# A transformer block on one core: the first LayerNorm in two halves of its slots, with shift, scale and w1 loaded and used in two halves of their columns

## The chip, the core and the metric

The kernel runs on one of the eight cores of a Trainium2 chip. The core has five engines with queues of their own: TensorE (PE, with weight loads shown as PEld), VectorE (DVE), ScalarE (ACT), GpSimd (POOL) and SyncE (SP), which here only issues DMAs. The metric is the device time of one execution in microseconds, as the median of several executions. All tensors are float32.

## The reference

A conditioned block: six rows per batch entry are made from the condition, and two residual branches use them as shift, scale and gate. The input x has 2 batch entries of 2048 rows with 512 features; the hidden width of the second branch is 1024.

```python
emb = jnp.dot(jax.nn.silu(t), ada_w) + ada_b
shift_msa, scale_msa, gate_msa, shift_mlp, scale_mlp, gate_mlp = jnp.split(emb, 6, axis=-1)
norm = _ln(x) * (1.0 + scale_msa[:, None]) + shift_msa[:, None]
h = jax.nn.gelu(jnp.dot(norm, ssm_w1) + ssm_b1, approximate=False)
ssm_out = jnp.dot(h, ssm_w2) + ssm_b2
x = x + gate_msa[:, None] * ssm_out
norm2 = _ln(x) * (1.0 + scale_mlp[:, None]) + shift_mlp[:, None]
hf = jax.nn.gelu(jnp.dot(norm2, ff_w1) + ff_b1, approximate=True)
ff_out = jnp.dot(hf, ff_w2) + ff_b2
x = x + gate_mlp[:, None] * ff_out
```

## The kernel before

**Tiling.** The 4096 rows are cut into 8 blocks of 512. A block holds 128 partitions with 4 rows each; the four rows of a partition are its slots. Features are cut into four chunks k of 128. The products of a block are formed in the way of Strassen and Winograd: seven products P1 to P7 of halves instead of eight, with sums of halves of the operands made beforehand by DVE or POOL. `group` (L376) issues the products in a given order; after each, `after` drains PSUM, and then the hooks hung on that product are issued. The schedule is manual: each engine works in the order in which the code issues to it.

**The beginning, by engine.** The first 16 us belong to block 0, before any product of a block can run.

- SP loads in this order: x of block 0 in two pieces, ada_0 (shift), ada_1 (scale), w1, ada_2 (gate), w2, b2, x of block 1, ada_3, ada_4, fw1 (L232 to L249). ada_0 to ada_4 are blocks of 512 columns of ada_w. ACT's queue loads the small rows with the condition and the biases.
- PE runs idle products (L774) and turns the small rows into columns (colsT). When ada_0 and ada_1 have landed, it forms shift and scale (`modulation`, L253, products at L261): for each, 16 small products, four at a time on column groups of the array. Between them and P1 stand 16 transposes (L494) of the normalized block.
- DVE forms the statistics of the four slots (L425, L426), copies colsT (L779), adds 1 to the scale's bias (L790), makes `pick` (L793) and `pick_bc` (L800), a selection matrix that the gate's product uses, and computes four small operations for the scales (L442 to L445) after POOL's two (L434, L436). It then turns and finishes shift (L271, L275), normalizes slots 1 and 3 (L469), finishes scale, and modulates chunks 1 and 3 (L510). ACT normalizes slots 0 and 2 (L465) and modulates chunks 0 and 2 (L508). Normalized rows go into the tile `blocks`, modulated ones into nT.
- POOL forms four sums of quarters of w1 (`sums_of_first` through `weight_of_first`, L311): w_s[1], then the quarter 21 in place, then w_s[0], then w_s[2]. DVE forms four sums of nT in the same way (`summed`, L530, L311): two before P1's drain, the third after P1, the fourth after P2.

**Block 0's first products** stand in the order P1, P2, P5, P6, P3, P7, P4 (L843). P1 uses the quarter 11 of w1 and P2 the quarter 12, both in the first half of w1's columns; P1 needs chunks 0 and 1 of nT, P2 chunks 2 and 3. P5 needs POOL's second sum and DVE's second sum, P6 POOL's third, P3 POOL's fourth. After P2, PE forms the gate's rows (`rows_of_gates`, L284, from ada_2); DVE adds the bias to them (grows, L293). After P5, PE multiplies grows by pick_bc (pgate, `make_gate`, L299); DVE multiplies b2 (gb, L830) and then w2 (L359) with pgate. DVE's order in this stretch is: sums 1 and 2, drain of P1 (forms, L565), sum 3, drain of P2 (L571), grows, sum 4, drain of P5, gb, w2, drain of P6.

Of the kernel before, what the change touches and what calls it, by code (L numbers as in the profile page):

```python
# [36 lines left out]
F32 = mybir.dt.float32  # L37
AF = mybir.ActivationFunctionType
ALU = mybir.AluOpType
EPS = 1e-06  # L40
# [100 lines left out]
def kernel(  # L141
# [16 lines left out]
    nc = tc.nc  # L158
    P = 128
    B, N, D = x.shape  # L160
    H = fw1.shape[1]
    KD = D // P
    KH = H // P
    C = 4
    TB = C * P
# [5 lines left out]
    const = ctx.enter_context(tc.tile_pool(name="const", bufs=1))  # L171
# [3 lines left out]
    small = ctx.enter_context(tc.tile_pool(name="small", bufs=3))  # L175
    ps_t = ctx.enter_context(tc.tile_pool(name="ps_t", bufs=2, space=bass.MemoryType.PSUM))
    ps_g = ctx.enter_context(tc.tile_pool(name="ps_g", bufs=2, space=bass.MemoryType.PSUM))
# [7 lines left out]
    G = 32  # L185
# [3 lines left out]
    R_COND, R_ADA = 0, B * KD  # L189
# [3 lines left out]
    def big_tile(name):  # L193
        return big.tile([P, KD, D], F32, tag="big", name=name)
# [3 lines left out]
    def load_x(i, pieces=1):  # L198
        xs[i] = big_tile(f"x_{i}")
        for s in range(pieces):  # L200
            c = slice(s * C // pieces, (s + 1) * C // pieces)
            nc.sync.dma_start(out=xs[i][:, c, :], in_=x_blk[i][:, c, :])

    ada = {}

    def load_ada(g):
        ada[g] = big_tile(f"ada_{g}")
        nc.sync.dma_start(
            out=ada[g], in_=ada_w[:, g * D : (g + 1) * D].rearrange("(k p) n -> p k n", p=P)
        )  # L210

    def load_w(name, w, t=None, eng=nc.sync):
        if t is None:
            t = const.tile([P, w.shape[0] // P, w.shape[1]], F32, tag=name, name=name)
        eng.dma_start(out=t, in_=w.rearrange("(k p) n -> p k n", p=P))
        return t
# [13 lines left out]
    ident = const.tile([P, P], F32, tag="ident", name="ident")  # L230
    make_identity(nc, ident)
    load_x(0, 2)  # L232
    load_ada(0)
    load_ada(1)
    w1_sb = load_w("w1", w1)
    load_ada(2)

    nc.gpsimd.memset(brows[:, :2, :], 0.0)
    for n, g in enumerate((2, 5)):
        nc.scalar.dma_start(  # L240
            out=brows[:B, n, :], in_=ada_b[g * D : (g + 1) * D].unsqueeze(0).to_broadcast([B, D])
# [6 lines left out]
    load_ada(4)  # L248
    fw1_sb = load_w("fw1", fw1)  # L249

    mods = {}

    def modulation(g0, part):  # L253


        g = g0 + part
        pa = ps_g.tile([P, D], F32, tag="x", name=f"pada_{g}")
        w = ada[g].rearrange("p k (n m q) -> p k m n q", n=KD, q=G)
        for k in range(KD):
            for m in range(P // G):  # L260
                nc.tensor.matmul(  # L261
                    pa[m * G : (m + 1) * G, :P],
                    silu[:, k, :],
                    w[:, k, m],
                    start=(k == 0),
                    stop=(k == KD - 1),
                    tile_position=(0, m * G),
                    skip_group_check=True,
                )
        turned = pa[:, P : 2 * P]  # L270
        nc.vector.transpose(turned, pa[:, :P])  # L271
        turned = turned.rearrange("p (n q) -> p n q", n=KD)
        m = const.tile([P, KD, B], F32, tag=f"mod_{g0}_{part}", name=f"mod_{g0}_{part}")
        bias = colsT[:, R_ADA + g * KD : R_ADA + (g + 1) * KD]
        nc.vector.tensor_tensor(m, turned[:, :, :B], bias.unsqueeze(2).to_broadcast([P, KD, B]), ALU.add)  # L275
        mods[g0, part] = m

    gate, gate_rows = {}, {}

# [23 lines left out]
    def quarters(lo, hi, a, b):  # L303

        return {"11": lo[:, :, a], "12": hi[:, :, a], "21": lo[:, :, b], "22": hi[:, :, b]}
# [7 lines left out]
    def sums_of_first(q, s, eng, cut=1):  # L313

        return [
            lambda: cut_sum(eng, s[1], q["11"], q["21"], ALU.subtract, cut),
            lambda: cut_sum(eng, q["21"], q["21"], q["22"], ALU.add, cut),
            lambda: cut_sum(eng, s[0], q["21"], q["11"], ALU.subtract, cut),
            lambda: cut_sum(eng, s[2], q["12"], s[0], ALU.subtract, cut),
        ]  # L320
# [10 lines left out]
    def first_operands(q, s):  # L331
        return {"P1": q["11"], "P2": q["12"], "P3": s[2], "P4": q["22"], "P5": q["21"], "P6": s[0], "P7": s[1]}
# [4 lines left out]
    def thirds(t):  # L337
        return [t[:, j] for j in range(3)]

    def weight_of_first(name, w_sb):  # L340

        K, M = w_sb.shape[1], w_sb.shape[2]
        tile_s = const.tile([P, 3, K // 2, M // 2], F32, tag=f"{name}_s", name=f"{name}_s")
        s = thirds(tile_s)
        lo, hi = w_sb[:, : K // 2, :], w_sb[:, K // 2 :, :]
        q = quarters(lo, hi, slice(0, M // 2), slice(M // 2, M))
        return first_operands(q, s), sums_of_first(q, s, nc.gpsimd), tile_s
# [64 lines left out]
    class Norm:  # L412
# [17 lines left out]
        def scales(self, on_dve=False):  # L430

            n, v = self.name, nc.gpsimd
            ve = small.tile([P, C], F32, tag="ve", name=f"ve{n}")
            v.tensor_scalar(ve, self.mv[:, :, 1], EPS, None, ALU.add)  # L434
            r = small.tile([P, C], F32, tag="r", name=f"r{n}")
            v.tensor_tensor(r, ve, minus_half, ALU.pow)  # L436
            e = small.tile([P, C], F32, tag="e", name=f"e{n}")
            self.rstd = small.tile([P, C], F32, tag="rstd", name=f"rstd{n}")
            self.nmr = small.tile([P, C], F32, tag="nmr", name=f"nmr{n}")
            if on_dve:  # L440
                v = nc.vector
                v.tensor_tensor(e, r, ve, ALU.mult)  # L442
                v.scalar_tensor_tensor(e, e, -0.5, r, ALU.mult, ALU.mult)
                v.scalar_tensor_tensor(self.rstd, e, 1.5, r, ALU.add, ALU.mult)
                v.scalar_tensor_tensor(self.nmr, self.mv[:, :, 0], -1.0, self.rstd, ALU.mult, ALU.mult)  # L445
                return
            v.tensor_tensor(e, r, r, ALU.mult)
            v.tensor_tensor(e, e, ve, ALU.mult)
            v.tensor_scalar(e, e, -0.5, 1.5, ALU.mult, ALU.add)
            v.tensor_tensor(self.rstd, r, e, ALU.mult)  # L450
            v.tensor_tensor(self.nmr, self.mv[:, :, 0], self.rstd, ALU.mult)
            v.tensor_scalar(self.nmr, self.nmr, -1.0, None, ALU.mult)  # L452

        def blocks(self):
            return work.tile([P, C, KD, C, Q], F32, tag="blocks", name=f"blocks{self.name}")
# [293 lines left out]
    def run(ops):  # L749
        for op in ops:  # L750
            op()
# [4 lines left out]
    n1 = {0: Norm(0, 1), 1: Norm(1, 1)}  # L756

    minus_half = const.tile([P, C], F32, tag="minus_half", name="minus_half")
# [6 lines left out]
    colsT = const.tile([P, ROWS], F32, tag="colsT", name="colsT")  # L765
# [5 lines left out]
    for n in range(IDLE):  # L771
# [3 lines left out]
            idle, ident, ident.unsqueeze(1).to_broadcast([P, C, P]), start=True, stop=True  # L775
        )

    run(n1[0].stats())
    nc.vector.tensor_copy(colsT, pt[:, :ROWS])  # L779


    nc.scalar.activation(
# [1 line left out]
        colsT[:, R_COND:R_ADA].rearrange("p (b k) -> p b k", b=B),  # L784
        AF.Silu,
    )

    for g in (1, 4):
        rows_g = colsT[:, R_ADA + g * KD : R_ADA + (g + 1) * KD]
        nc.vector.tensor_scalar(rows_g, rows_g, 1.0, None, ALU.add)  # L790

    pick = const.tile([P, B], F32, tag="pick", name="pick")
    nc.vector.tensor_reduce(  # L793
# [4 lines left out]
    )  # L798
    pick_bc = const.tile([P, B, P], F32, tag="pick_bc", name="pick_bc")
    nc.vector.tensor_copy(pick_bc, pick.unsqueeze(2).to_broadcast([P, B, P]))  # L800
    n1[0].scales(on_dve=True)

    w1_ops, w1_sums, _ = weight_of_first("w1", w1_sb)
    run(w1_sums)
    modulation(0, 0)
    for c in range(C):
        n1[0].normal(c, nc.vector if c % 2 else None, on_pe=True)
    modulation(0, 1)
    pts = {}

    def transposed(k):
        pts[k] = n1[0].transpose(k, ps_g.tile([P, TB], F32, tag="yv"[k % 2], name=f"pt1_0_{k}"))

    for k in range(KD):
        transposed(k)
    for k in range(KD):
        n1[0].modulate(k, pts[k], nc.vector if k % 2 else None)
    n1_sums = n1[0].summed(nc.vector)
    run(n1_sums[:2])
    load_ada(5)  # L820
    fw2_sb = load_w("fw2", fw2)
    gb, hA = {2: b2_bc}, {}
# [15 lines left out]
    st = n1[1].stats()  # L838
    hook(hooks, ("P5",), [ssm_gate, gb2_0] + biases(0, b2_bc) + fold2(0, 1))
    hook(hooks, ("P6",), fold2(1, 7))  # L840
    hook(hooks, ("P3", "P7"), st[:2])
    hook(hooks, ("P7",), [lambda: modulation(3, 0)])
    hA[0] = First(0, n1[0].ops, hooks, ("P1", "P2", "P5", "P6", "P3", "P7", "P4"), hA_0)  # L843
    w2_ops = found["w2"][0]
# [9 lines left out]
    st = n2[0].stats()  # L854
# [17 lines left out]
    n1_sums = n1[1].summed(nc.vector)  # L872
# [21 lines left out]
    st = n1[2].stats()  # L894
# [221 lines left out]
```

## Time and profile before

| | us |
|---|---|
| median of 3 runs | 600.43 |
| lowest and highest | 600.42 and 600.75 |
| the profiled execution, whole | 600.48 |
| its span, first to last instruction | 598.7 |
| PE busy in the span | 591.4 |
| DVE busy | 374.3 |
| POOL busy | 399.1 |
| ACT busy | 218.8 |

The span is 1.8 us shorter than the profiled execution, which is near the median. The granted TensorE clock was 0.999 of full speed. In the lines of the profile a timeline row gives the start in us, the length in us, the engine, the line of the code, the operation, and the tiles as out<-in; a bracket gives how long the engine was idle before and what released it. A row of the chain of waits gives start, length and what the chain ran through; it is followed backwards from the last instruction, at each step to what released it.

### The profile page before, as it was taken

The numbers are of one execution on the slowest core, as the hardware profiler recorded it, in microseconds if no ns is written. First come the engines' busy times: TensorE is split into PE (matmuls) and PEld (weight loads), VectorE is DVE, ScalarE is ACT, GpSimd is POOL, SyncE is SP. The second block draws the span as 40 slices with busy tenths as digits, with TensorE's granted clock in tenths as the row PEclk, the third lists the DMA queues.
The fourth block names the chain that finished last, engine by engine and source line by source line (L and its number), as shares of the span: only waits on it lengthen the run. The fifth ranks groups of instructions, "written<-read, shape, count | busy, mean of one in ns | idle before, by whom it ended". The sixth has DMA issues, their size and how long they took to land.

```text
span 598.7 us, 8148 instructions
## 1 busy us (share of the span) xinstructions
PE 591.4 (99%) x2827; PEld 510.1 (85%) x2827; DVE 374.3 (63%) x638; ACT 218.8 (37%) x363; POOL 399.1 (67%) x465
## 2 busy tenths in 40 slices
PE   8999999999999999999999999999999999999997
PEld 4787888888888888888888888888888888888886
DVE  5978988897654475555754468654565346467642
ACT  3234247305432364133721346123553225212420
POOL 2878689999743995549968498886984695540110
PEclk9999999999999999999999999999999999999999
DMA  8990222300213004340052601321020300022001
GB/s 320 412 359 10 62 68 78 102 36 36 70 72 117 25 1 121 119 129 2 14 143 65 213 8 36 106 71 71 1 65 7 106 35 1 2 58 84 0 1 70
DMA packets 23116, 49.31 MB, mean 82 GB/s; under 512 B 4340, under 2 KB 4896, under 8 KB 22180
## 3 DMA queue, kind: packets, MB, share of 16 engines
q1 hardware_dynamic: 20032, 44.58, 22.2%
q10 hardware_dynamic: 3044, 4.23, 2.7%
q8 instruction: 22, 0.36, 0.2%
q14 instruction: 18, 0.15, 0.1%
HBM read 25.72 MB, written 8.39 MB: 57 GB/s over the span
## 4 chain that ended last, share of the span: by engine, by line
PE 94%; DMA 2%; POOL 1%; DVE 1%; ACTq 1%; ACT 1%; issue 0%; SPq 0%
PE py_oC L391 18%; PE px_hC L712 10%; PE pv_oC L391 9%; PE py_hA L391 9%; PE py_oA L391 8%; PE py_hC L712 8%; PE pv_hC L712 8%; PE px_oC L391 5%; PE pv_hA L391 4%; PE pv_oA L391 4%; PE px_hA L391 2%; PE py_hC L391 2%; PE px_oA L391 2%; DMA ada<-in_L_cond_ada_w_dram 2%; PE pv_hC L391 1%; PE pt L494 1%
## 5 line engine op out<-in xcount | busy, mean ns | idle before, releaser
L625 POOL TENSOR_TENSOR x<-x,gb 128x512 f32<-128x512 f32 x64 | 79.9, 1282 | 9.3 <-DVE gb L869 3.5
L508 ACT ACTIVATE nT<-nT,mod,mod 128x512 f32<-128x512 f32 x54 | 39.6, 803 | 102.9 <-DMA nT<-blocks 102.9
L311 POOL TENSOR_TENSOR hSC<-hClo 128x512 f32<-128x512 f32 (+1 forms) x34 | 40.1, 1183 | 42.9 <-ACT hClo L707 38.7
L465 ACT ACTIVATE nT<-x,nmr,rstd 128x512 f32<-128x512 f32 x56 | 42.4, 803 | 58.4 <-POOL nmr L452 42.6
L434 POOL TENSOR_SCALAR ve<-mv 128x4 f32<-128x4 f32 x16 | 3.7, 232 | 85.8 <-DVE mv L426 85.5
L391 PE MATMUL py_oC<-fw_s,hSC 128*128 128x256 f32 x256 | 57.9, 379 | 0.0
L391 PEld LDWEIGHTS py_oC<-fw_s,hSC 128*128 128x128 f32 x256 | 48.6, 190 | 6.6
L613 DVE TENSOR_TENSOR x<-py_oC,x 128x512 f32<-128x512 f32 (+1 forms) x36 | 22.5, 629 | 40.4 <-PE py_oC L391 40.3
L425 DVE BATCH_NORM_STATS2 st<-x 128x6 f32<-128x512 f32 x64 | 43.4, 678 | 5.0 <-DMA x<-in_x_dram 4.8
L712 PE MATMUL py_hC<-forms,fw 128*128 128x256 f32 x168 | 40.8, 379 | 0.0
L476 DVE STREAM_TRANSPOSE blocks<-nT 128x512 f32<-128x512 f32 x56 | 37.8, 694 | 3.8 <-ACT nT L465 3.4
L729 DVE TENSOR_TENSOR hClo<-hClo,py_hC 128x512 f32<-128x512 f32 x42 | 28.4, 681 | 16.6 <-ACT hClo L726 10.4
L650 POOL TENSOR_TENSOR forms<-forms 128x256 f32<-128x256 f32 x48 | 35.5, 740 | 2.8
L712 PEld LDWEIGHTS py_hC<-forms,fw 128*128 128x128 f32 x168 | 31.8, 190 | 4.4
L613 DVE TENSOR_TENSOR x<-py_oA,x 128x512 f32<-128x512 f32 x32 | 22.0, 689 | 19.5 <-PE py_oA L391 19.0
L729 DVE TENSOR_TENSOR hChi<-hChi,pv_hC 128x512 f32<-128x512 f32 x35 | 23.4, 684 | 17.1 <-PE pv_hC L712 17.1
L391 PE MATMUL py_oA<-w_s,hSA 128*128 128x256 f32 x128 | 30.4, 381 | 0.2 <-DVE x L613 0.2
L391 PE MATMUL py_hA<-nS,w_s 128*128 128x256 f32 x128 | 30.4, 381 | 0.0
L707 ACT ACTIVATE hClo<-hClo,colsT 128x256 f32<-128x256 f32 x56 | 25.4, 500 | 10.8 <-DVE hClo L729 10.7
L391 PE MATMUL py_oC<-fw,hClo 128*128 128x256 f32 x128 | 28.9, 379 | 0.0
L391 PE MATMUL pv_oC<-fw,hClo 128*128 128x256 f32 x128 | 28.9, 379 | 0.0
L391 PE MATMUL pv_oC<-fw,hSC 128*128 128x256 f32 x128 | 28.9, 379 | 0.0
(210 smaller groups left out, 1405.6 us busy)
## 6 DMA issues: line engine op xcount, KB each, us to landing
nT<-blocks SPq DMA_DIRECT2D x168, 64.0 KB, 2.0
out_dram<-x SPq DMA_DIRECT2D x15, 512.0 KB, 3.2
x<-in_x_dram SPq DMA_DIRECT2D x7, 1024.0 KB, 7.3
ada<-in_L_cond_ada_w_dram SPq DMA_DIRECT2D x6, 1024.0 KB, 9.5
fw<-in_L_cond_ff_w_dram SPq DMA_DIRECT2D x3, 2048.0 KB, 9.1
nT<-blocks ACTq DMA_DIRECT2D x56, 64.0 KB, 2.0
w<-in_L_cond_ssm_w_dram SPq DMA_DIRECT2D x3, 1024.0 KB, 7.5
x<-in_x_dram SPq DMA_DIRECT2D x2, 512.0 KB, 5.1
```

The costliest lines, as they stand in the source:

```text
L311: eng.tensor_tensor(out[:, r], a[:, r], b[:, r], f)
L391: nc.tensor.matmul(ps[b][j * apart][:, j, :], lhs(p, j, k), rhs(p, j, k), start=(fresh and j * (not apart) == 0 and k == 0), stop=(p in (" ...
L425: nc.vector.bn_stats(st, xs[self.i][:, c, :])
L465: nc.scalar.activation(t, x_c, AF.Identity, bias=self.nmr[:, c : c + 1], scale=self.rstd[:, c : c + 1])
L476: nc.vector.transpose(self.bl[:, :, :, c, :].rearrange("p m k q -> p k m q"), self.nT[:, c, :].rearrange("p (k m q) -> p k m q", k=KD, m=C),)
L508: nc.scalar.activation(dst, src, AF.Identity, bias=shift, scale=scale)
L613: nc.vector.tensor_tensor(d, ps[BANK[p]][:, js], d, ALU.add)
L625: lambda c=c: nc.gpsimd.tensor_tensor(xs[i][:, c, :], xs[i][:, c, :], gb, ALU.add)
L650: eng.tensor_tensor(reg[d], reg[a], reg[b], ALU.add if f == "+" else ALU.subtract)
L707: nc.scalar.activation(h, h, AF.Gelu_apprx_tanh, bias=fb1T[:, m : m + 1])
L712: nc.tensor.matmul(ps[b][:, j, :], fa[ra][:, j * P : (j + 1) * P], fb[rb].rearrange("p a (c q) -> p c a q", q=Q), start=(fresh and j == 0) ...
L729: nc.vector.tensor_tensor(dest(d), dest(d), ps[b], op)
```

## The change

ada_0, ada_1 and w1 are loaded in two halves of their columns: first halves of ada_0 and ada_1, second halves of both, then w1's two halves. Shift and scale are formed in two halves of their chunks: `modulation` takes a half, issues PE's products for it, and returns the DVE part as a function `finish` that is called later. The scales of block 0's first norm are formed for slots 0 and 1 and for slots 2 and 3 apart (`scales_of`). ACT normalizes slots 0 and 1, DVE slots 2 and 3. PE's order becomes: first halves of shift and scale, all chunks' transposes of slots 0 and 1, those of slots 2 and 3, second halves of shift and scale, P1. Chunks 0 and 1 are modulated before the second halves are finished, chunks 2 and 3 after. `pick` and `pick_bc` move on DVE from before the scales to after the first two sums of nT.

```diff
-    def load_ada(g):
-        ada[g] = big_tile(f"ada_{g}")
+    def load_ada(g, half=None):
+        if not half:
+            ada[g] = big_tile(f"ada_{g}")
+        c = slice(0, D) if half is None else slice(half * D // 2, (half + 1) * D // 2)
         nc.sync.dma_start(
-            out=ada[g], in_=ada_w[:, g * D : (g + 1) * D].rearrange("(k p) n -> p k n", p=P)
+            out=ada[g][:, :, c], in_=ada_w[:, g * D : (g + 1) * D][:, c].rearrange("(k p) n -> p k n", p=P)
         )
...
-    load_ada(0)
-    load_ada(1)
-    w1_sb = load_w("w1", w1)
+    for half in range(2):
+        load_ada(0, half)
+        load_ada(1, half)
+    w1_sb = const.tile([P, KD, D], F32, tag="w1", name="w1")
+    for c in (slice(0, D // 2), slice(D // 2, D)):
+        nc.sync.dma_start(out=w1_sb[:, :, c], in_=w1[:, c].rearrange("(k p) n -> p k n", p=P))
...
-    def modulation(g0, part):
+    def modulation(g0, part, half=None):
...
         g = g0 + part
-        pa = ps_g.tile([P, D], F32, tag="x", name=f"pada_{g}")
+        if not half:
+            pada[g] = ps_g.tile([P, D], F32, tag="x", name=f"pada_{g}")
+            mods[g0, part] = const.tile([P, KD, B], F32, tag=f"mod_{g0}_{part}", name=f"mod_{g0}_{part}")
+        n = slice(0, KD) if half is None else slice(half * KD // 2, (half + 1) * KD // 2)
+        pa = pada[g][:, n.start * G : n.stop * G]
...
+        def finish():
+            nc.vector.transpose(turned, pa)
+            to = mods[g0, part][:, n]
+            by_n = turned.rearrange("p (n q) -> p n q", q=G)
+            nc.vector.tensor_tensor(
+                to, by_n[:, :, :B], bias.unsqueeze(2).to_broadcast([P, n.stop - n.start, B]), ALU.add
+            )
...
+        def scales_of(self, s):
...
+            ve, r, e = [small.tile([P, C], F32, tag=k, name=f"{k}{n}")[:, s] for k in ("ve", "r", "e")]
+            nc.gpsimd.tensor_scalar(ve, self.mv[:, s, 1], EPS, None, ALU.add)
+            nc.gpsimd.tensor_tensor(r, ve, minus_half[:, s], ALU.pow)
+
+            def rest():
+                v.tensor_tensor(e, r, ve, ALU.mult)
+                v.scalar_tensor_tensor(e, e, -0.5, r, ALU.mult, ALU.mult)
+                v.scalar_tensor_tensor(self.rstd[:, s], e, 1.5, r, ALU.add, ALU.mult)
+                v.scalar_tensor_tensor(
+                    self.nmr[:, s], self.mv[:, s, 0], -1.0, self.rstd[:, s], ALU.mult, ALU.mult
+                )
...
-    run(n1[0].stats())
+    halves = slice(0, C // 2), slice(C // 2, C)
+    st = n1[0].stats()
+    run(st[:2])
+    scales_lo = n1[0].scales_of(halves[0])
+    run(st[2:])
     nc.vector.tensor_copy(colsT, pt[:, :ROWS])
+    scales_hi = n1[0].scales_of(halves[1])
+    scales_lo()
...
+    for c in (0, 1):
+        n1[0].normal(c, on_pe=True)
...
+    scales_hi()
+    for c in (2, 3):
+        n1[0].normal(c, nc.vector, on_pe=True)
+    w1_ops, w1_sums, _ = weight_of_first("w1", w1_sb)
+    run(w1_sums)
...
+    for finish in [modulation(0, part, 0) for part in range(2)]:
+        finish()
+    for k in range(KD):
+        transposed(k, (0, 1))
+    for k in range(KD):
+        transposed(k, (2, 3))
+    finish_hi = [modulation(0, part, 1) for part in range(2)]
+    n1[0].modulate(0, pts[0])
+    n1[0].modulate(1, pts[1], nc.vector)
+    run(finish_hi)
+    n1[0].modulate(2, pts[2])
+    n1[0].modulate(3, pts[3], nc.vector)
+    n1_sums = n1[0].summed(nc.vector)
+    run(n1_sums[:2])
 
     pick = const.tile([P, B], F32, tag="pick", name="pick")
     nc.vector.tensor_reduce(
...
     nc.vector.tensor_copy(pick_bc, pick.unsqueeze(2).to_broadcast([P, B, P]))
-    n1[0].scales(on_dve=True)
-
-    w1_ops, w1_sums, _ = weight_of_first("w1", w1_sb)
-    run(w1_sums)
-    modulation(0, 0)
-    for c in range(C):
-        n1[0].normal(c, nc.vector if c % 2 else None, on_pe=True)
-    modulation(0, 1)
-    pts = {}
-
-    def transposed(k):
-        pts[k] = n1[0].transpose(k, ps_g.tile([P, TB], F32, tag="yv"[k % 2], name=f"pt1_0_{k}"))
-
-    for k in range(KD):
-        transposed(k)
-    for k in range(KD):
-        n1[0].modulate(k, pts[k], nc.vector if k % 2 else None)
-    n1_sums = n1[0].summed(nc.vector)
-    run(n1_sums[:2])
```

More of the change, by code (lines that the diff above doesn't have):

```diff
@@ L249 @@
     fw1_sb = load_w("fw1", fw1)
-    mods = {}
-    def modulation(g0, part):
+    mods, pada = {}, {}
+    def modulation(g0, part, half=None):
         g = g0 + part
-        pa = ps_g.tile([P, D], F32, tag="x", name=f"pada_{g}")
+        if not half:
[3 more added lines that the diff above has]
+        pa = pada[g][:, n.start * G : n.stop * G]
         w = ada[g].rearrange("p k (n m q) -> p k m n q", n=KD, q=G)
@@ L261, in modulation @@
                 nc.tensor.matmul(
-                    pa[m * G : (m + 1) * G, :P],
+                    pa[m * G : (m + 1) * G, :],
                     silu[:, k, :],
-                    w[:, k, m],
+                    w[:, k, m, n],
                     start=(k == 0),
@@ L269, in modulation @@
                 )
[L270 to L276, printed above, removed]
+        turned = pada[g][:, P + n.start * G : P + n.stop * G]
+        bias = colsT[:, R_ADA + g * KD : R_ADA + (g + 1) * KD][:, n]
+        def finish():
[5 more added lines that the diff above has]
+            )
+        if half is not None:
+            return finish
+        finish()
     gate, gate_rows = {}, {}
@@ L452, in scales @@
             v.tensor_scalar(self.nmr, self.nmr, -1.0, None, ALU.mult)
+        def scales_of(self, s):
+            n, v = f"{self.name}_{s.start}", nc.vector
+            if s.start == 0:
+                self.rstd = small.tile([P, C], F32, tag="rstd", name=f"rstd{self.name}")
+                self.nmr = small.tile([P, C], F32, tag="nmr", name=f"nmr{self.name}")
+            ve, r, e = [small.tile([P, C], F32, tag=k, name=f"{k}{n}")[:, s] for k in ("ve", "r", "e")]
[8 more added lines that the diff above has]
+                )
+            return rest
         def blocks(self):
@@ L790, with transposed @@
         nc.vector.tensor_scalar(rows_g, rows_g, 1.0, None, ALU.add)
+    scales_hi()
[3 more added lines that the diff above has]
+    run(w1_sums)
+    pts = {k: ps_g.tile([P, TB], F32, tag="yv"[k % 2], name=f"pt1_0_{k}") for k in range(KD)}
+    def transposed(k, slots):
+        for c in slots:
+            nc.tensor.transpose(pts[k][:, c * P : (c + 1) * P], n1[0].xn[:, c, k * P : (k + 1) * P], ident)
+    for finish in [modulation(0, part, 0) for part in range(2)]:
+        finish()
+    for k in range(KD):
[10 more added lines that the diff above has]
+    run(n1_sums[:2])
     pick = const.tile([P, B], F32, tag="pick", name="pick")
```

## The prediction

> **What bounds the kernel now.** I read the page first: busy shares and the chain that ended last.
>
> ```profile
> span 598.7 us, 8148 instructions
> PE 591.4 (99%) x2827; PEld 510.1 (85%) x2827; DVE 374.3 (63%) x638; ACT 218.8 (37%) x363; POOL 399.1 (67%) x465
> PE 94%; DMA 2%; POOL 1%; DVE 1%; ACTq 1%; ACT 1%; issue 0%; SPq 0%
> ```
>
> TensorE is the bound almost everywhere. The changed code runs in the first 16 us, so the next view is the chain in order of time, cut to 0 to 60 us.
>
> ```profile
> 2.10 9.47 DMA ada<-in_L_cond_ada_w_dram
> ...
> 11.62 1.08 PE pada L261 x32
> 12.70 1.90 PE pt L494 x16
> 14.60 1.88 PE py_hA L391 x8
> ...
> 19.20 1.93 PE pv_hA L391 x8
> 21.13 0.88 PE pgate L299 x2
> 22.01 1.74 PE py_hA L391 x8
> ...
> 23.77 0.69 DVE forms L565
> ```
>
> The chain starts with the landing of ada_1 (11.58), runs over PE, and at 23.77 turns to DVE until P4 starts at 28.30. From 28.30 to 59.70 it is PE without a gap, then an ACT, DMA and POOL tail that this PE work releases; from 76.65 to the last matmul it is PE alone. So what P4 gains or loses at 28.30 should reach the end whole. Third view: the timeline of 8 to 21 us, which shows what the chain hides.
>
> ```profile
> 8.59 0.29 DVE L800 COPY pick_bc<-pick 128x256 f32<-128x256 f32 x1
> ...
> 14.45 1.27 POOL L311 TENSOR_TENSOR w_s<-w 128x512 f32<-128x512 f32 x1 [4.95 <-DMA w<-in_L_cond_ssm_w_dram]
> 15.55 0.72 DVE L311 TENSOR_TENSOR nS<-nT 128x512 f32<-128x512 f32 x1
> 15.80 1.59 POOL L311 TENSOR_TENSOR w<-w 128x512 f32<-128x512 f32 x1
> 16.31 1.64 DVE L311 TENSOR_TENSOR nT<-nT 128x512 f32<-128x512 f32 x1
> 17.48 1.61 POOL L311 TENSOR_TENSOR w_s<-w 128x512 f32<-128x512 f32 x1
> 17.87 0.68 DVE L565 TENSOR_TENSOR forms<-py_hA,colsT 128x512 f32<-128x512 f32 x1
> 18.47 1.16 DVE L311 TENSOR_TENSOR nS<-nT 128x512 f32<-128x512 f32 x1
> 19.16 1.60 POOL L311 TENSOR_TENSOR w_s<-w,w_s 128x512 f32<-128x512 f32 x1
> 20.16 0.67 DVE L293 TENSOR_TENSOR grows<-pada,brows 128x512 f32<-128x512 f32 x1
> ```
>
> DVE and POOL take turns: whenever both add two SBUF tiles, one waits out the other. The ends run 15.72 (POOL), 16.27 (DVE), 17.39, 17.95, 19.09, 19.63, 20.76: a DVE sum ends 0.55 after the POOL sum before it, a POOL sum 1.13 after the DVE sum. The forms add at 17.87, which reads PSUM, is not held (0.68). So DVE's row up to grows, whose end (20.83) just fits under pgate (21.13), hangs on POOL's first sum, and that on w1's landing.
>
> [...] no copy lies beside a POOL sum in this trace. [...] In 15 to 20 us the trace has 409 GB/s with 2 KB rows, 80 ns a row on each of 16 engines[...]. No run here shows half-row loads.
>
> **The change part by part.**
>
> Loads. Six half loads replace three, 3 MB in all at 409 GB/s, 7.7 us[...]. Bounds 0 and +2.5 (a third slower[...]); I take 0.4. The three more issues on SP (0.4 each) run while the queues are full. First halves of ada_0 and ada_1 together land when ada_0 did, 9.2 plus 0.1; ada_1's second half at 11.9; w1's first half near 13.3, all of w1 at 14.85. ada_2 (estimate 17.2 before, from w1 at 14.4 and ada_1 to ada_3 at 2.8 us per MB) comes at 17.6.
>
> Statistics in halves. POOL gets slots 0 and 1 at 6.46 and is done by 7.9 (0.23 and 1.05 as before; two columns may be cheaper, but DVE is busy to 8.2 anyway). Four small DVE operations at 0.2 end at 8.9, so ACT normalizes slots 0 and 1 from 8.95 to 10.5 (1.52 for two) instead of from 10.33. The upper half's scales end at 10.29 as the whole did, and DVE normalizes slots 2 and 3 from 10.33 to 11.35 (0.99 before, at 10.84).
>
> PE. First-half shift and scale are done by about 10.2. Sixteen transposes start at 10.5 instead of 12.70 and take 1.90, to 12.4. Then come the second halves. A half product is not in the trace; 32 records took 1.08, so between 0.54 and 1.08, and I take 0.65: 13.05 and 13.6.
>
> DVE. After its normals it finishes the first halves: four operations, a half transpose between 0.17 (the tiniest operation) and 0.33 (the whole), the add 0.17; about 0.9, to 12.2. Modulation writes nT, and in the built program nT takes ada_0's buffer: modulate(0) and (1) wait until PE has read ada_0's second half, 13.1, against 13.39 and 13.77. DVE then does modulate(1) (0.81), four more finishing operations (0.85), modulate(3) (0.81): its first sum of nT is ready to start at 15.6. Before it was 15.55. The head start on PE (P1 at 13.95 against 14.60) is spent on DVE's doubled finishing.
>
> The lock. POOL's first sum needs both halves of w1: 14.85 to 16.12. DVE, ready at 15.6, waits, and ends at 16.67; POOL 17.79; DVE 18.35; POOL's third sum takes the pair until 19.49. Now pick, pick_bc follow on DVE, moved from idle time at 8.4 to here. [...] pick_bc [...] waits for 19.49: it ends at 19.65 and holds the in-order queue, forms among it. Nothing covers it here. POOL's fourth sum goes next and ends at 20.78; DVE's third sum, ready at 20.2 after forms, waits for it: 21.33. Then forms (to 21.9), grows (to 22.5), and pgate can start at 22.6 against 21.13: +1.5. As a formula: pgate moves by 1.1 plus the delay of w1.
>
> PE waits there; P5 (18.7 to 20.6) is long done. P6, gb, the w2 folds and P4 follow pgate in the old distances. b2 (landed 21.43, from issue to landing 13.2) plus 0.4 is before the new gb at 23.5; ada_3 (26.4) plus 0.4 before PE needs it. Sum: 600.48 for the profiled execution plus 1.5; against the median, 600.43, it is 601.9.
>
> **The rivals.** (a) The copy is not held by POOL. Then pick_bc costs 0.5, DVE's third sum ends at 20.04, grows at 21.2, pgate 21.3: +0.2, 600.6. For it: no copy beside a POOL sum in this trace. [...]
> (b) POOL wins the pair twice: if DVE gets to its first sum after POOL's first has ended (16.1), POOL's second starts, and DVE ends at 17.9 instead of 16.7; the copy is then caught behind the last sum. +2.2, 602.6. It needs DVE 0.5 later than I have it, or 0.2 later and w1 not delayed.
> (c) Half rows are a third slower. b2 then lands near 24, gb waits on it (22.05 before), and ada_3 near 29 holds PE: +2.0, 602.4.
> (d) The other side: the head start survives on DVE. Place: DVE's first sum. If it starts before POOL's (14.85, so 0.75 earlier than I have it, with finishing operations that overlap and half products at 0.54), one turn of the lock is saved, and if the copy slips through too, pgate waits only for P5, which the gate rows' product (L284) holds until ada_2 is there at 17.6: P5 ends at 20.55, -0.6, 599.8. It decides from a start below 14.85; later, the lock order is the one above.
>
> **How the numbers follow.** Main case 0.52, (a) 0.18, (b) 0.13, (c) 0.08, (d) 0.09. The main case's own range is 601.5 (no delay of w1) to 602.4 (0.8 us). 0.2%, 1.2 us, is about what a measurement of this kernel can tell from no change; slower by more is the main case with w1 at least 0.1 late (0.45 of its 0.52), (b) and most of (c): 0.65. Within 0.2%: the rest of it, (a), and nearly all of (d): 0.31. Faster: 0.04. The range reaches from (a) with some of (d) to beyond (b): 600.2 to 603.0.
>
> **What would show it.** pick_bc on DVE about 1 us long and ending just after a POOL sum; pgate near 22.6; ACT's normals near 9; transposes near 10.5; the first DVE sum near 15.6 and held. Wrong if pick_bc takes 0.3 among POOL's sums (then a), if w1's halves land after 15.6 (then c or another order), or if pgate starts before 21.1 (then d).

## The result and the profile after

| | before | changed |
|---|---|---|
| median of 11 runs each, us | 600.64 | 602.05 |
| ratio, 95% interval | | 1.0021 [1.0011, 1.0031] |
| the profiled execution, us | 600.48 | 602.06 |
| its span, us | 598.7 | 600.3 |

The changed kernel is slower by 0.21%, 1.3 us with an interval of 0.7 to 1.9; the profiled executions differ by 1.58 us. The prediction was 1.5, and 601.9 for the median. In part of the executions of kernels that begin like the kernel before, and in one of the changed kernel, TensorE's granted clock was 0.996 or 0.997 over the run and the time some 0.8 to 2.9 us longer, so the medians of the experiments below are taken over executions at 0.999 or 1.0, while their ratios and intervals are over all executions.

First the page of the changed kernel, the lines that were shown of the kernel before:

```profile
span 600.3 us, 8296 instructions
PE 591.7 (99%) x2891; PEld 510.1 (85%) x2891; DVE 376.8 (63%) x646; ACT 218.7 (36%) x363; POOL 399.0 (66%) x467
PE 93%; DVE 3%; POOL 1%; DMA 1%; ACT 1%; issue 1%; ACTq 1%; DVEq 0%
```

PE's busy time grew by 0.3 us and the span by 1.6: PE was not given more work, it waited. DVE's share of the chain went from 1% to 3%. The chain of waits of the changed kernel in order of time, cut to the first stage (start, length, what):

```profile
10.49 1.86 PE pt L846 x15
12.35 0.63 PE pada L270 x32
13.00 0.81 DVE nT L546
14.58 0.82 DVE nT L546
15.50 1.42 DVE nS L327
16.94 1.64 DVE nT L327
18.69 1.18 DVE pick_bc L871
19.87 0.60 DVE forms L601
...
22.13 0.69 DVE grows L309
22.86 1.12 PE pgate L315 x2
```

Before, the chain ran over PE from 11.62 to 23.77 (P1, P2, P5, pgate, P6). Now it leaves PE at 13.0 and stays on DVE until pgate, with pick_bc in the middle. The timeline of the same stretch, with POOL beside it, tells what DVE waited for:

```profile
13.83 1.99 PE L407 MATMUL py_hA<-nT,w 128*128 128x256 f32 x8 [0.45 <-ACT nT L544]
...
15.10 1.27 POOL L327 TENSOR_TENSOR w_s<-w 128x512 f32<-128x512 f32 x1 [5.83 <-DMA w<-in_L_cond_ssm_w_dram]
...
15.50 1.41 DVE L327 TENSOR_TENSOR nS<-nT 128x512 f32<-128x512 f32 x1
...
18.11 1.61 POOL L327 TENSOR_TENSOR w_s<-w 128x512 f32<-128x512 f32 x1
...
18.69 1.18 DVE L871 COPY pick_bc<-pick 128x256 f32<-128x256 f32 x1
18.73 1.06 PE L300 MATMUL pada<-ada,silu 128*32 128x512 f32 x8 [1.18 <-DMA ada<-in_L_cond_ada_w_dram]
...
19.80 1.26 POOL L327 TENSOR_TENSOR w_s<-w,w_s 128x512 f32<-128x512 f32 x1
...
20.39 1.22 DVE L327 TENSOR_TENSOR nS<-nT 128x512 f32<-128x512 f32 x1
...
22.86 1.12 PE L315 MATMUL pgate<-grows,pick_bc 128*128 128x512 f32 x2 [1.14 <-DVE grows L309]
```

P1 starts 0.77 us earlier than in the chain of before (13.83 for 14.60). Then DVE's first sum, started at 15.50, takes 1.41 instead of 0.72 and ends at 16.91, 0.54 after POOL's first (late by 0.65 with w1), which ends at 16.37. pick_bc takes 1.18 instead of 0.29 and ends at 19.87, 0.15 after POOL's third sum (19.72). POOL's fourth sum then goes ahead, DVE's third ends at 21.61 instead of 19.63, and pgate starts 1.73 later than in the chain of before, PE idle for 1.14 us before it. The end of grows moves from 20.83 to 22.81, by 1.98, and P6 and P4 (30.28 for 28.30) by the same 1.98. P6 of the second hidden product (py_hC) is only 1.62 later, and the span is 1.6 longer.

### The profile page after: what moved, and what is told of

Its sections match the earlier page's. It is cut to its first block, busy times and chain, and to the rows that moved or that the text cites. A ratio compares the mean times of both kernels' runs of the same rounds, so it can differ in the third digit from the quotient of the medians.

```text
span 600.3 us, 8296 instructions
## 1 busy us (share of the span) xinstructions
PE 591.7 (99%) x2891; PEld 510.1 (85%) x2891; DVE 376.8 (63%) x646; ACT 218.7 (36%) x363; POOL 399.0 (66%) x467
## 4 chain that ended last, share of the span: by engine, by line
PE 93%; DVE 3%; POOL 1%; DMA 1%; ACT 1%; issue 1%; ACTq 1%; DVEq 0%
PE py_oC L407 18%; PE px_hC L748 10%; PE pv_oC L407 9%; PE py_hA L407 9%; PE py_oA L407 8%; PE py_hC L748 8%; PE pv_hC L748 8%; PE px_oC L407 5%; PE pv_hA L407 4%; PE pv_oA L407 4%; PE py_hC L407 2%; PE px_oA L407 2%; PE px_hA L407 2%; PE pv_hC L407 1%; DMA x<-in_x_dram 1%; PE pgate L315 1%
## 5 line engine op out<-in xcount | busy, mean ns | idle before, releaser
L407 PE MATMUL px_oC<-fw,hChi 128*128 128x256 f32 x128 | 28.9, 379 | 0.0
```

The source lines that it names most:

```text
L407: nc.tensor.matmul(ps[b][j * apart][:, j, :], lhs(p, j, k), rhs(p, j, k), start=(fresh and j * (not apart) == 0 and k == 0), stop=(p in (" ...
```

## The experiments

Times in us; "less before" is the median less that of the kernel before on the same chip (600.58 to 600.61; 600.64 for the changed kernel, 600.66 for e12), "P6 of hC" the start of that product in the profile. The starts of products are those of the chain of waits, in which a product starts when the one before it has ended; in a timeline the start can stand up to 0.2 earlier, since matmuls overlap (the eight of P1 before, of 0.38 each, take 1.97). The starts of e11 are from its second profile.

| kernel | median (executions) | less before | pgate | P6 | P4 | P6 of hC |
|---|---|---|---|---|---|---|
| before | | | 21.13 | 22.01 | 28.30 | 76.65 |
| changed | 602.05 (10) | +1.4 | 22.86 | 23.99 | 30.28 | 78.27 |
| e1 pick early | 600.81 (14) | +0.2 | 21.99 | 22.85 | 29.14 | 77.16 |
| e2 pick late, in before | 601.92 (10) | +1.3 | 22.22 | 23.35 | 29.64 | 77.96 |
| e11 the same, pick in PSUM | 600.79 (9) | +0.2 | 21.32 | 22.34 | 28.63 | 76.96 |
| e3 half loads, in before | 601.12 (8) | +0.5 | 21.48 | 22.61 | 28.90 | 76.95 |
| e4 w1 by rows | 601.25 (14) | +0.6 | 22.08 | 23.20 | 29.50 | 77.54 |
| e5 e1 with w1 by rows, third sum later | 600.48 (13) | -0.1 | 21.61 | 22.47 | 28.76 | 76.77 |
| e8 gate rows late | 601.02 (13) | +0.4 | 22.87 | 20.94 | 28.89 | 77.22 |
| e10 and statistics late | 600.95 (14) | +0.4 | 22.84 | 20.91 | 28.09 | 77.19 |
| e9 three more DMAs, in before | 600.39 (10) | -0.2 | 21.23 | 22.22 | 28.51 | 76.61 |
| e12 e5 with w2's load held | 600.37 (13) | -0.3 | 21.38 | 22.24 | 28.54 | 76.56 |

**e1: the copy moved away, in the changed kernel.**

```diff
+    pick = const.tile([P, B], F32, tag="pick", name="pick")
...
     halves = slice(0, C // 2), slice(C // 2, C)
     st = n1[0].stats()
...
     run(n1_sums[:2])
-    pick = const.tile([P, B], F32, tag="pick", name="pick")
...
```

> The changed kernel with pick and pick_bc made by DVE before the first statistics, where DVE waits for x; all else as in the changed kernel. Lock theory (pick_bc caught behind POOL's third sum of w1 costs the most, the later w1 the rest): pick_bc takes 0.3 us, DVE's third sum ends near 20.3 instead of 21.6, grows near 21.5, pgate starts at 21.5 to 21.8 (22.86 in the changed kernel, 21.13 before), and the time is 0.4 to 0.8 us above the kernel before, so 0.9 to 1.3 us below the changed kernel. Rival (DVE's doubled finishing of shift and scale, or the later transfers, cost the time and the copy only fills a wait that is there anyway): pgate stays near 22.8 and the time 1.4 to 1.6 us above before.

The timeline of e1:

```profile
18.15 1.60 POOL L327 TENSOR_TENSOR w_s<-w 128x512 f32<-128x512 f32 x1
...
19.14 1.16 DVE L327 TENSOR_TENSOR nS<-nT 128x512 f32<-128x512 f32 x1
...
20.82 0.68 DVE L309 TENSOR_TENSOR grows<-pada,brows 128x512 f32<-128x512 f32 x1
```

Without the copy in between, DVE's third sum gets the turn after POOL's third and ends at 20.30 (expected 20.3), grows at 21.50, as with the lock theory. Ratio 1.0000 [0.9993, 1.0008]; by the medians, moving the copy and its small reduction takes back 1.2 us of the 1.4. The halves' doubled finishing is still there, so it is not what cost the time. pgate comes 0.2 later than expected, for P5 now ends after grows: the gate rows' product before it waited 1.37 for ada_2 and started at 19.00. The time is 0.2 below what was expected; of the 0.84 at P4, 0.33 is made up in the tail (e9 below).

**e2: the same move alone, in the kernel before.**

```diff
-    pick = const.tile([P, B], F32, tag="pick", name="pick")
...
     n1[0].scales(on_dve=True)
...
     run(n1_sums[:2])
+    pick = const.tile([P, B], F32, tag="pick", name="pick")
...
```

> The kernel before, with only one edit: pick and pick_bc stand after DVE's first two sums of nT instead of before the scales. Lock theory: pick_bc becomes about 1 us long, ends just after a POOL sum (near 19.2), POOL's fourth sum then goes ahead of DVE's third (which ends near 20.9 instead of 19.6), pgate starts near 22.2 instead of 21.13, and the time rises by 0.9 to 1.3 us. Rival (the copy costs only its own 0.45 us and the rest of the changed kernel's loss is from the loads and the halves): the time rises by 0.3 us or less.

The timeline of e2:

```profile
17.48 1.60 POOL L311 TENSOR_TENSOR w_s<-w 128x512 f32<-128x512 f32 x1
...
18.06 1.17 DVE L819 COPY pick_bc<-pick 128x256 f32<-128x256 f32 x1
...
19.16 1.26 POOL L311 TENSOR_TENSOR w_s<-w,w_s 128x512 f32<-128x512 f32 x1
19.75 1.22 DVE L311 TENSOR_TENSOR nS<-nT 128x512 f32<-128x512 f32 x1
```

pick_bc ends at 19.23, 0.15 after POOL's sum; DVE's third sum ends at 20.97 and pgate starts at 22.22, as expected. Ratio 1.0020 [1.0012, 1.0029]: the moved copy alone costs about as much as the whole change, in which 0.36 is made up later (e9).

**e11: the same place, but a copy that reads PSUM.** e2 with `pick` in PSUM:

```diff
-    pick = const.tile([P, B], F32, tag="pick", name="pick")
+    pick = ps_t.tile([P, B], F32, tag="t", name="pick")
```

> The kernel e2_pick_late (the kernel before with pick and pick_bc after DVE's first two sums of nT) with one edit: pick lies in PSUM instead of SBUF, so that the copy reads PSUM like the drains, which no POOL sum holds. Lock theory: pick_bc starts near 18.0, takes 0.3 to 0.5 instead of 1.17 us and does not end with a POOL sum; POOL's third sum still ends near 19.1, DVE's third sum is there in time for the turn that it has in the kernel before and ends near 19.7, grows near 21.0, pgate starts at 21.2 to 21.5, and the time is 0.1 to 0.4 us above before. Rival (the place in DVE's queue costs the time, not the pair): pick_bc stays long or the time 0.9 us or more above before.

In the profile of this run TensorE's clock was down to 0.50 for a while (last section), PE and DVE were late, and no POOL sum lay beside the copy. A second profile of it:

> The kernel of e11_pick_late_psum once more, for a profile at full clock (that of e11 fell in an execution in which TensorE's clock was 0.5 between 12.7 and 14.6 us, so that no POOL sum lay beside the copy). Lock theory as for e11: pick_bc near 18.0 beside POOL's third sum of w1, 0.3 to 0.5 us long, pgate at 21.2 to 21.5. Rival as for e11: pick_bc near 1.2 us long or pgate above 22.

The timeline of the second profile:

```profile
17.75 1.61 POOL L311 TENSOR_TENSOR w_s<-w 128x512 f32<-128x512 f32 x1
...
18.34 0.42 DVE L819 COPY pick_bc<-pick 128x256 f32<-128x256 f32 x1
...
19.28 0.68 DVE L311 TENSOR_TENSOR nS<-nT 128x512 f32<-128x512 f32 x1
```

In the middle of POOL's sum (17.75 to 19.36) the copy takes 0.42, DVE's third sum gets its turn before POOL's fourth, and pgate starts at 21.32. The time is 1.1 below e2's, from a tile's place alone: what costs the time is that the copy is held by POOL's sum, not its position in the queue. For the same 256 elements the copy took 1.17 in e2 with `pick` in SBUF, beside a POOL sum, and 0.29 in the kernel before, with no POOL sum beside it. "Lock" and "the pair" in the recorded texts stand for these turns of DVE and POOL; what in the hardware makes them was not shown.

**e3: the loads alone, in the kernel before.** Six half loads as in the changed kernel; products and norm as before.

> The kernel before, with only the loads changed: shift, scale and w1 come in two halves of their columns (1 KB rows), in the changed kernel's order, and are used whole. Lock theory: w1 is there 0.65 us later (POOL's first sum at 15.1 instead of 14.45), every turn of DVE and POOL moves by that, pgate starts near 21.8, and the time rises by 0.4 to 0.7 us. Rival (the transfers are hidden, the pair of engines catches up): pgate within 0.2 us of 21.13 and the time within 0.2 us.

The timeline of e3:

```profile
15.05 1.27 POOL L316 TENSOR_TENSOR w_s<-w 128x512 f32<-128x512 f32 x1 [5.39 <-DMA w<-in_L_cond_ssm_w_dram]
...
20.76 0.67 DVE L298 TENSOR_TENSOR grows<-pada,brows 128x512 f32<-128x512 f32 x1
```

w1 is 0.60 late and grows ends 0.60 late (21.43 for 20.83). By the chain pgate starts only 0.35 later, since in the kernel before the chain came to it at the end of P5 (21.13) and not of grows; but P6 and P4 are 0.60 later, like grows, so nothing is gained by that. Ratio 1.0007 [0.9997, 1.0018]: not told apart from no change by the interval, though the trace shows the shift.

Together: the end of grows moves by 1.35 in e2 and by 0.60 in e3, in sum 1.95; in the changed kernel it moves by 1.98. P6 of hC moves by 1.31 and 0.30, in sum 1.61, and by 1.62 in the changed kernel. So next to nothing is left for the halves of the norm, for which the change is made, in either direction.

**e4: POOL's sums earlier.** The changed kernel with w1 loaded in halves of its rows (the quarters 11 and 21 lie in the lower rows).

```diff
-    for c in (slice(0, D // 2), slice(D // 2, D)):
-        nc.sync.dma_start(out=w1_sb[:, :, c], in_=w1[:, c].rearrange("(k p) n -> p k n", p=P))
+    for k in range(0, KD, KD // 2):
+        nc.sync.dma_start(
+            out=w1_sb[:, k : k + KD // 2, :],
+            in_=w1[k * P : (k + KD // 2) * P, :].rearrange("(k p) n -> p k n", p=P),
+        )
```

> The changed kernel, with w1 loaded in two halves of its rows (2 KB rows[...]) instead of its columns. POOL's first sum needs only the lower rows, so it can start near 13.4 and be done before DVE is ready; the pair then meets first at POOL's second sum. Lock theory: one turn is saved: POOL's third sum ends near 18.1 and its fourth near 19.7, pick_bc ends just after one of these, DVE's third sum ends near 20.6 instead of 21.6, pgate starts near 21.8, and the time is 0.4 to 0.9 us above before. Rival (what counts is when DVE gets to its first sum, not when POOL does): pgate stays near 22.8, 1.3 to 1.6 us above before.

The timeline of e4:

```profile
13.45 1.27 POOL L330 TENSOR_TENSOR w_s<-w 128x512 f32<-128x512 f32 x1 [4.04 <-DMA w<-in_L_cond_ssm_w_dram]
...
17.87 1.60 POOL L330 TENSOR_TENSOR w_s<-w,w_s 128x512 f32<-128x512 f32 x1
...
18.45 1.17 DVE L874 COPY pick_bc<-pick 128x256 f32<-128x256 f32 x1
...
20.15 0.68 DVE L330 TENSOR_TENSOR nS<-nT 128x512 f32<-128x512 f32 x1
```

One turn is saved, as expected: the copy is now caught behind POOL's fourth sum instead of its third, and DVE's third (0.68), with no POOL sum beside it, ends at 20.83 instead of 21.61. pgate is at 22.08 (21.8 expected).

**e5: three edits together.** e1 with w1 by rows, and DVE's third sum after grows:

```diff
-    hook(hooks, ("P1",), n1_sums[2:3])
-    hook(hooks, ("P2",), [lambda: rows_of_gates(2)] + n1_sums[3:])
+    hook(hooks, ("P2",), [lambda: rows_of_gates(2)] + n1_sums[2:])
```

> The changed kernel with three edits: pick and pick_bc before the statistics, w1 in two halves of its rows, and DVE's third sum of nT after grows instead of ahead of it. Lock theory: DVE's second sum ends near 18.3, the drains of P1 and P2 follow at once and grows ends near 20.2, 0.6 ahead of the kernel before; then DVE is no longer what pgate waits for. What is late next by the traces is the gate rows' product, which waits for ada_2 until 18.65 (in the kernel before PE reached it at 18.14 by its own order), so P5 runs from 19.7 to 21.6 and pgate starts near 21.6, P6 near 22.5 (22.01 before), the time 0.0 to 0.4 us above before. Rival (the head start on PE reaches pgate once DVE is freed): pgate starts below 21.0 and the time is 0.3 to 0.7 us below before.

The timeline of e5:

```profile
18.62 1.06 PE L303 MATMUL pada<-ada,silu 128*32 128x512 f32 x8 [1.06 <-DMA ada<-in_L_cond_ada_w_dram]
...
19.61 1.99 PE L410 MATMUL pv_hA<-nT,w 128*128 128x256 f32 x8
19.74 0.69 DVE L312 TENSOR_TENSOR grows<-pada,brows 128x512 f32<-128x512 f32 x1
```

grows ends at 20.43, 0.40 before that of the kernel before, and pgate is not earlier: PE waited 1.06 for ada_2, so P5 holds it until 21.61, as expected. The head start is spent on the third transfer instead. The ratio is 0.9985 [0.9976, 0.9994], but the medians of the table differ by only 0.1 us, and in the profiles P6 of hC starts 0.12 later than before. So it is level with the kernel before, and not shown to be faster.

**e8 and e10: past ada_2.** e8 has the edits of e1 and e4, forms the gate rows after P5 and pgate after P6, with POOL's sums of w1 in two pieces each; e10 also moves a statistic of block 1 behind the drain of P7.

```diff
+    hook(hooks, ("P5",), [lambda: rows_of_gates(2)] + n1_sums[3:])
+    hook(hooks, ("P6",), [ssm_gate, gb2_0] + biases(0, b2_bc) + fold2(0, 1))
...
-    hook(hooks, ("P3", "P7"), st[:2])
+    hook(hooks, ("P7",), st[:2])
```

> The changed kernel with pick and pick_bc early, w1 in halves of its rows, POOL's four sums of w1 in two pieces each, and the gate rows' product (with grows and DVE's fourth sum) after P5 instead of P2 and pgate with gb and the first w2 fold after P6 instead of P5. If PE's own order of work is what is left (theory: after the pair and the late ada_2 are out of the way, PE has no gap from P1 on), DVE's second sum ends near 17.9, P5 starts near 17.9 instead of 19.2, P6 near 20.8 instead of 22.0, and P4 0.2 to 0.5 us earlier than before (28.30): the time is 0.2 to 0.8 us below before. Rival (DVE is full in this stretch, so an earlier PE only waits for its drains): P4 at 28.3 or later, the time equal to before or up to 0.5 us above.

> The kernel e8_gate_rows_late with one edit: the statistics of block 1's first slot on DVE after the drain of P7 instead of ahead of it (28.18 to 28.84 there), where P4 waited 0.70 for that drain. If DVE's order alone kept the earlier PE work from paying, P4 starts near 28.2 (28.89 in e8, 28.30 before), P6 of the second hidden product near 76.2 to 76.3 (76.65 before), and the time is 0.2 to 0.5 us below before. If DVE is simply full there, P4 stays above 28.6 and the time within 0.3 us of before.

The timeline of e8, then that of e10:

```profile
20.87 1.99 PE L410 MATMUL py_hA<-nS,w_s 128*128 128x256 f32 x8
...
28.89 1.99 PE L410 MATMUL py_hA<-nS,w 128*128 128x256 f32 x8 [0.70 <-DVE forms L617]
```

```profile
28.09 1.99 PE L410 MATMUL py_hA<-nS,w 128*128 128x256 f32 x8
...
38.71 1.99 PE L410 MATMUL py_oA<-w_s,hSA 128*128 128x256 f32 x8 [0.70 <-DVE x L652]
```

In e8 P6 is 1.07 earlier than before, and P4 0.59 later, since it waits for the drain of P7. e10 frees that drain, P4 is 0.21 earlier than before, and ten microseconds on PE waits 0.70 for another drain. In both, DVE sums of the next product start near 29.95 (29.40 before): between 19.6 and 23.8 DVE is idle for 1.46 us in e8 while it waits for PE's new order (0.35, 0.33, 0.61 and 0.17), and its work is done later. The rival of e8 came true, and of e10's expectation only the start of P4: its time is 0.4 above before, not 0.2 to 0.5 below. These kernels differ from e5 in several edits at once, so what each of them did is not told apart.

**e12: do the later loads delay ada_2?** e5 with w2's load, and those behind it, held until 12.3.

> The kernel e5_all_three with one edit: the loads behind ada_2 in the queue (w2, b2, block 1's x, ada_3, ada_4, fw1) are not issued before DVE has written one column of w2's tile, ahead of its first modulation (near 12.3 us, where it waits for PE; w2's load was issued at 9.3 in e5). If these loads take bandwidth from ada_2, it lands at 17.6 or earlier instead of 18.6, the gate rows' product follows P2 without a gap, pgate starts at 20.5 to 20.9 (21.45 in e5), P4 at 27.7 to 28.2, and the time is 0.4 to 0.9 us below before, the best of the series. If the transfers stand in order, ada_2 lands at 18.6 again and the time is that of e5; if the later loads are then too late (b2 for gb near 22.5), it is above before.

The gate rows started at 18.39 instead of 18.62, not at 17.6: the later loads take little. Ratio 0.9991 [0.9983, 0.9999], the lowest median of the series, but 0.1 below e5 is less than what e5's own executions spread (599.67 to 600.78). Why ada_2 is there so late stays open: in the changed kernel, e1, e4, e5 and e12 the gate rows' product waits for it until 18.39 to 19.00, while in e3, whose six half loads are those of the changed kernel, the product starts at 18.35 without waiting for it.

**e9: the missing 0.36.** P4 was 1.98 late in the changed kernel, P6 of hC 1.62. The kernel before, with ada_4 in four pieces:

```diff
-    load_ada(4)
+    ada[4] = big_tile("ada_4")
+    for k in range(KD):
+        nc.sync.dma_start(out=ada[4][:, k, :], in_=ada_w[k * P : (k + 1) * P, 4 * D : 5 * D])
```

> The kernel before with only one edit: the load of ada_4, which nothing waits for in the first 60 us, in four pieces instead of one, so that three more DMAs are issued ahead of those of nT at 58 to 65 us, as in the changed kernel. It asks why 1.98 us of delay at P4 became 1.62 at P6 of the second hidden product (76.65 before). Theory (ACT passes a fixed row of waits for nT's DMAs[...] and the place in the row of the DMA that lands last depends on the count of DMAs issued before): ACT's idle time ahead of its modulation of nT falls from 6.02 to 5.7 us, P6 of hC starts 0.3 us earlier and the time is 0.2 to 0.4 us below before. Rival (the 0.3 us is from the later start itself, slack in DVE's and ACT's work between 28 and 66 us): nothing moves, the time is within 0.1 us of before.

ACT's modulation after the DMAs of nT, in the timelines of the kernel before, of e9 and of the changed kernel:

```profile
66.56 2.93 ACT L508 ACTIVATE nT<-nT,mod,mod 128x512 f32<-128x512 f32 x4 [6.02 <-DMA nT<-blocks]
```

```profile
66.53 2.93 ACT L510 ACTIVATE nT<-nT,mod,mod 128x512 f32<-128x512 f32 x4 [5.76 <-DMA nT<-blocks]
```

```profile
68.20 2.93 ACT L544 ACTIVATE nT<-nT,mod,mod 128x512 f32<-128x512 f32 x4 [5.72 <-DMA nT<-blocks]
```

In e9 P4 is 0.21 later than before and P6 of hC 0.04 earlier: 0.25 is made up there, and the idle time falls from 6.02 to 5.76. The time is 0.2 below before; its ratio, 1.0001 [0.9990, 1.0012], doesn't tell it from no change. ACT's idle time ahead of this modulation is 5.72 to 5.76 in all nine kernels with three more DMAs (changed, e1, e3, e4, e5, e8, e9, e10, e12) and 6.02 or 6.03 in those without (before, e2, e11). So it goes with the three more DMAs, and not with a later start: e2 and e11 are 1.34 and 0.33 late at P4 and keep the 6.02. The distance from P4 to P6 of hC is 48.32 to 48.35 in the three without and 47.99 to 48.10 in seven of the nine; in e8 and e10 it is 48.33 and 49.10, and e10 has the wait of 0.70 shown above in between. The place in a row of waits as the cause was not tried by itself. It fits that ACT's four extra wait records ended at 66.5 in the kernel before, right ahead of the modulation, and at 65.9 in e9, well ahead of it.

## Why the prediction was right

The case that came is the main one, and the steps came in its order.

- **The copy.** Held behind POOL's third sum, ending 0.15 after it, then POOL's fourth sum ahead of DVE's third: all as predicted, shown by e1, e2 and e11. That the copy would be held was the author's assumption, which no trace of before showed; in the changed kernel it took 1.18. A copy that is not held, as in rival (a), is what e11 makes by hand: +0.2. (a) was given the same size, but with a later w1 and a shorter copy, so that the two agree is chance.
- **DVE's halves.** The half product was put at 0.65 and took 0.63; transposes at 10.5 and 10.49; the first sum at 15.6 and 15.50. POOL's power on two columns took 0.74, not 1.05, which brought DVE's normals to 10.09; they end in the wait for PE's second halves all the same. Rival (d), the head start that survives, needed DVE at its first sum before POOL, which was put at 14.85 and came at 15.10; DVE came at 15.50, 0.40 too late.
- **The term that was too small: the delay of w1.** 0.4 was taken, the author's assumption, as no run of before had half rows, and 0.65 came between the two profiles. Over all profiles POOL's first sum starts at 14.45 to 14.64 with whole rows of ada_0, ada_1 and w1 (before, e2, e9, both of e11) and at 15.05 to 15.13 with half rows (changed, e1, e3), 0.57 apart on average. Each later step, from the first sum's end to pgate, missed by 0.22 to 0.31, and the prediction's own formula for pgate, 1.1 plus the delay of w1, gives 1.75 with the measured delay, where 1.73 came. That the half loads delay w1 is shown by e3; how they do it is not. The 7.7 us were reckoned with 409 GB/s, the rate of 15 to 20 us. In 9 to 15 us the kernel before did not reach it throughout (first two lines before, then two changed; length, busy PE, PEld, DVE, ACT and POOL with counts, granted clock, DMA share, GB/s):

```profile
9.00:12.00 3.00, 1.49 (x49) 1.22 (x52) 2.06 (x8) 1.52 (x2) 0.50 (x1) 1.00 1.00 373
12.00:14.40 2.40, 2.40 (x44) 2.16 (x32) 1.13 (x3) 0.97 (x2) 0.00 (x0) 1.00 1.05 408
```

```profile
9.00:12.00 3.00, 2.67 (x66) 2.22 (x56) 2.35 (x11) 1.44 (x2) 0.27 (x1) 1.00 1.09 385
12.00:15.00 3.00, 2.55 (x73) 2.11 (x72) 1.89 (x6) 1.20 (x2) 0.00 (x0) 1.00 1.09 383
```

From 9 to 14.4 us the kernel before moved 388 GB/s on average and the changed one 382, which over 2.1 MB is less than 0.1 us. So the measured rates leave most of the delay of w1 unexplained.

- **A slack that was not there, and a tail that was left out, of opposite sign.** The prediction had grows 1.67 later (22.5) and pgate 1.5 later, as if 0.2 were lost in the wait for P5 before. The runs show no such slack: P6 and P4 move as far as the end of grows does, within 0.01, in e11 (0.33), e3 (0.60), e4 (1.20), e2 (1.35) and the changed kernel (1.98). In the chain this shows as a pgate of 1.12 instead of 0.88, as its start no longer overlaps the end of P5: +0.24. And 0.36 is made up between P4 and P6 of hC, where the prediction had P4's delay reach the end whole; in e9 the three extra DMAs make up 0.25. 1.5, 0.25 for the later w1 and 0.24 give the 1.98 at P4 within 0.01; less 0.36, 1.62. That the total came so near is luck: these errors nearly cancel.
- **ada_2** was put at 17.6, and its product waited for it until 18.73. In the changed kernel that is covered (P5 ends at 21.7, pgate waits for grows until 22.8); e1 and e5 show that it is the next thing late.

## What to carry to other kernels

When an instruction is moved, ask whether an engine with which it takes turns is at work at the new place: beside a sum of POOL, a 0.29 us copy on DVE cost 1.2 us here, by its own wait and by the turn that it lost for the next sum (an estimate from e2: that sum would end 0.8 us later if it ran at once in 0.68 from 19.75, and the lost turn adds 0.5). Moving the copy to idle time gave the time back, and so, nearly, did its source in PSUM. The head start on the bounding engine did not pay, since the other inputs of the next products did not come earlier as well: here the second operand's sums, a third transfer and the drains each took it in turn.

## What was not expected of the hardware

TensorE's clock fell to half, 0.50, near the start of the execution in the first profile of e11; the columns of these stretches are the length, busy times of PE, PEld, DVE, ACT and POOL with counts, the granted clock, the DMA share and GB/s:

```profile
8.00:12.00 4.00, 1.80 (x42) 1.08 (x44) 2.38 (x11) 1.73 (x3) 1.29 (x2) 0.99 1.04 389
11.00:12.70 1.70, 0.94 (x21) 0.93 (x25) 0.73 (x2) 0.80 (x2) 0.00 (x0) 0.78 1.04 389
12.70:14.60 1.90, 1.90 (x24) 1.52 (x14) 0.50 (x2) 0.00 (x0) 0.10 (x1) 0.50 1.05 387
```

In the first stretch PE is busy for 1.80 of 4 us, as it waits for ada_0 and ada_1. PE's longest wait there was 1.54 us, before the products of 11.77. PE's share of this stretch does not decide alone: in the profile of e3 it is 1.78 of the same 4 us, and the clock stayed at 1.00. From 14.6 to 17 us the clock was 0.84 on average; if it was either full or half, it was down for 3.4 us, from 11.95 to 15.37 (an estimate from the averages of 0.78, 0.50 and 0.84). 3.4 us at half make 0.997 over 601.7 us, which is the clock that this execution shows over the run. What brought the clock down was not shown. A clock of 0.996 or 0.997 over the run came in 23 of 121 executions of the kernel before beside the experiments and in 18 of 56 of e2, e3, e9 and e11. Of the seven kernels with the new first stage, where PE is busy for 3.3 to 3.8 us of these four (2.49 in the profile of before), it came in 1 of 92 executions. So the change makes the time steadier while it makes it longer. That the fuller PE is the cause was not tried alone.
